# Layer norms cut into quarters and channels, a written order for the first attention, and other buffers for the weights of a four-layer network

## The chip, the cores and the metric

The kernel runs on one core of one Trainium2 chip. The metric is the device time of one execution in microseconds (us), taken as the median of several executions. The engines are TensorE (PE, matmuls; its weight loads are shown as PEld), VectorE (DVE), ScalarE (ACT), GpSimd (POOL), and SyncE (SP), which issues all DMA transfers of this kernel. Each engine runs its own instructions in one fixed order, and waits at an instruction until what it needs is there; whatever stands behind the waiting instruction waits too.

## What is computed

There are 8 sequences of 112 tokens with 512 channels (x), and 8 context sequences of 375 tokens. All arithmetic is fp32. Four layers follow each other:

```python
# layer 0: cross attention of one head, residual scaled by alpha
x = x + alpha * (softmax((x @ w_q.T) @ (ctx @ w_k.T).T / sqrt(512)) @ (ctx @ w_v.T)) @ w_o.T
# layers 1 and 2: a recurrent (RWKV) layer each
xa = layernorm(x); sx = previous_token(xa) - xa
w, k, v, r, g = five data-dependent mixes of xa and sx, times Wk, Wv, Wr, Wg and a decay
y = recurrence over the tokens, 32 heads of 16          # "time mix"
x = x + (groupnorm(y) * silu(g)) @ Wo.T
xc = layernorm(x); sxc = previous_token(xc) - xc        # "channel mix"
x = x + sigmoid((xc + sxc * m_r) @ Wfr.T) * (relu((xc + sxc * m_k) @ Wfk.T) ** 2 @ Wfv.T)
# layer 3: two cross attentions of 16 heads of 128, each behind a layernorm, then an MLP behind a layernorm
```

## The kernel before, in words

**Layout.** Activations are kept turned: the 512 channels as 4 chunks of 128 partitions, the 896 tokens along the free dimension, and worked on in two halves of 448 tokens (`h` = 0 and 1). One product of a 128x128 weight block with 448 tokens is two PE instructions in the profile; a projection of one half and one output chunk is 4 such products.

**Who sets the order.** The program is written in Tile, whose scheduler reorders the instructions of each engine; only in a block under `tc.manual_schedule` do PE, DVE, ACT and POOL keep the written order. Before, only the recurrence (L682) is such a block. DMAs all go through SP in one order.

**Layer 0** (L224 to L356). The attention is folded: `w_qk` = w_q turned times w_k turned, and `w_vo` = w_v turned times w_o (`product`, L296, whose output ACT copies out of PSUM at L305). Then for each of 8 sequences `b`: PE turns the context into `rows` (3 tiles, copied by DVE), makes the scores `sc` (L336), DVE and ACT make the softmax, PE turns the probabilities (`pt`, copied by DVE into `pts`), and multiplies (`av`). For every second sequence, `park` (L251) forms sums and differences of the two contexts that later layers use: DVE copies (L261) and POOL subtractions (L263) fill a tile, and five DMAs (L268) put 2.6 MB of it into DRAM. Contexts live in 4 buffers, so the later ones are loaded when earlier ones are done with. The output projection `ps_o` is added to x by DVE (L353).

**Between the layers.** `values()` (L823) is a generator of independent matmuls (`ps_vk`, L933: the value products of layer 3's attentions) that other code uses to fill PE while it waits: `fill(n)` takes n pieces of it. Its weights are loaded at the end of layer 0 (`wv`, L842), combined by POOL (L849 to L852), and DVE subtracts two biases (`over`, L979). Constants (`ones_t`, `pick`, `mean_h`, `less_mean_h`) are made just before layer 1 (L797 to L816).

**A layer norm** (`layer_norm_half`, L166) of one half: partial sums over the chunks by DVE (L178, L180), mean over channels by PE (L182), subtraction by DVE (L187), square by ACT (L189), partial sums and PE again for the variance, square root by ACT (L194), then on DVE one reciprocal of 128x448 (L195) and one multiplication of all 4 chunks, 128x1792 (L196), then 4 scalings by ACT (L202). There are 14 of these half norms. `fills` says how many pieces of filler are put behind the mean, the square and the variance.

**Layers 1 and 2.** Weights rotate through 4 buffers (`weight`, L124): a new weight's DMA starts once the last reader of the old one in its buffer is done. In the time mix the order of loading is Wg, Wv, Wk, Wr (`"gvkr"`); Wg and Wv are then reordered in place, half by half, by an ACT copy (L419, `turng`, `turnv`) and a DVE copy back (L420). The channel mix (L723) has one pool for its norm output, mixes, `kk` and `rr`; its three projections are `fk`, `fr` and `fv`; for `fv` DVE multiplies (L772) and POOL adds to x (L773).

**The way into layer 3.** The last channel mix runs its `fv` half by half, and starts the first norm of layer 3 for half 0 (`y_ln3`, without scaling) while half 1 is being multiplied. Layer 3 scales that half (L202) and norms half 1, with the first key projections as filler: `ps_k1k` and `ps_k5k` (L1166), which need the weight wk, sums of it by POOL (`wsk`, L1067 to L1070), and the parked tiles `cs`, `cx` and `cy` (loaded at L1221 to L1228).

Of the kernel before, what the change touches and what calls it, by code (L numbers as in the profile page):

```python
# [22 lines left out]
F32 = mybir.dt.float32  # L23
# [85 lines left out]
def tile_kernel(ctx: ExitStack, tc: tile.TileContext, d: dict, out: bass.AP):  # L109
# [26 lines left out]

    mean_c = const.tile([P, P], F32, name="mean_c")
# [28 lines left out]
    def layer_norm_half(ps, work, y, h, scale, offset, name, room=None, bank=None, fills=(2, 2, 4), small_tag="rstd"):  # L166
# [22 lines left out]
        nc.scalar.activation(sq, y, AF.Square)  # L189
        fill(fills[1])  # L190
        var = over_channels(sq, "var")
        fill(fills[2])
        rstd = small("rstd", "")
        nc.scalar.activation(rstd, var, AF.Sqrt, bias=eps)  # L194
        nc.vector.reciprocal(rstd, rstd)  # L195
        nc.vector.tensor_mul(y, y, rstd.unsqueeze(1).to_broadcast([P, NC, NH]))  # L196
        if scale is not None:
            scale_by_channel(y, y, scale, offset)
# [23 lines left out]


    def layer0():  # L224
# [3 lines left out]
        with (  # L228

            tc.tile_pool(name="a0s", bufs=2, space=PSUM) as ps2,  # L230
            tc.tile_pool(name="a0c", bufs=4) as near,
            tc.tile_pool(name="a0", bufs=1) as keep,
# [18 lines left out]
            def park(b, c1, c2):  # L251
# [7 lines left out]
                for k in range(2):  # L259
                    for y, z in ((b11, c11), (b21, c21), (b22, c22)):  # L260
                        nc.vector.tensor_copy(y[:, k], z[:, k])  # L261
                    for y, z, less in ((t0, c12, c11), (t1, c22, t0), (t2, c22, c12), (t3, c21, t1)):
                        nc.gpsimd.tensor_sub(y[:, k], z[:, k], less[:, k])  # L263
# [22 lines left out]
            def turned(w, name):  # L286

                t = keep.tile([P, NC, C], F32, tag="turned", bufs=3, name=f"t_{name}")
                for o in range(NC):
                    p = mm(ps, f"ps_t{name}_{o}")  # L290
                    for k in range(NC):
                        nc.tensor.transpose(p[:, k * P : (k + 1) * P], w[:, k, o * P : (o + 1) * P], ident)
                    (nc.vector.tensor_copy if o % 2 else nc.scalar.copy)(t[:, o, :], p)
                return t

            def product(a, b, name, pool, scale=1.0):  # L296

                y = pool.tile([P, NC, C], F32, tag=name, name=name)
# [9 lines left out]
            w_qk = product(turned(w_q, "q"), turned(w_k, "k"), "w_qk", keep, 1.0 / math.sqrt(C))  # L308
            q = keep.tile([P, NC, N], F32, name="q0")
            z = last.tile([P, NC, N], F32, name="z0")  # L310
            project(
                ps,
                w_qk,
                lambda k, h: halves(x[:, k, :], h),
                lambda o, h, p: nc.scalar.copy(halves(q[:, o, :], h), p),
                "q0",
            )
            w_vo = product(turned(w_v, "v"), w_o, "w_vo", last)
            for b in range(B):
                tok = slice(b * L, (b + 1) * L)  # L320
                if b + 1 < B:
                    context(b + 1)
                cx = cxs[b]
                if b % 2:
                    park(b, cxs.pop(b - 1), cxs.pop(b))
                rows = work.tile([CT, 3, C], F32, tag="rows", name=f"rows0_{b}")
                for t in range(3):
                    p = mm(ps, f"ps_r0_{b}_{t}")[:CT, :]
                    for k in range(NC):
                        nc.tensor.transpose(  # L330
                            p[:, k * P : (k + 1) * P], cx[:, k, t * CT : (t + 1) * CT], ident
                        )
                    nc.vector.tensor_copy(rows[:, t, :], p)
                sc = ps2.tile([L, S], F32, tag="sc", name=f"sc0_{b}")
                for k in range(NC):
                    nc.tensor.matmul(sc, q[:, k, tok], cx[:, k, :], start=k == 0, stop=k == NC - 1)  # L336
                prob = softmax(work, sc, S, f"0_{b}")
                pt = ps2.tile([CT, 3, L], F32, tag="pt", name=f"pt0_{b}")
                for t in range(3):
                    nc.tensor.transpose(pt[:, t, :], prob[:, t * CT : (t + 1) * CT], ident[:L, :L])  # L340
                pts = work.tile([CT, 3, L], F32, tag="pts", name=f"pts0_{b}")
                nc.vector.tensor_copy(pts, pt)
                av = ps2.tile([P, NC, L], F32, tag="av", name=f"av0_{b}")
                for o in range(NC):
                    for t in range(3):
                        nc.tensor.matmul(
                            av[:, o, :], rows[:, t, o * P : (o + 1) * P], pts[:, t, :], start=t == 0, stop=t == 2
                        )
                nc.scalar.copy(z[:, :, tok], av)
# [33 lines left out]
    def time_mix_inputs(n, pre, names, ones_t, first, k, v, r, g, decay, rows):  # L383
# [7 lines left out]
        with (  # L391
# [21 lines left out]
            ws = {f: weight(f"{pre}W{f}") for f in "gvkr"}  # L413
# [309 lines left out]
    def channel_mix(n, pre, names, first):  # L723
        nonlocal filler
        with (
            tc.tile_pool(name=f"c{n}", bufs=1) as one,
            tc.tile_pool(name=f"cw{n}", bufs=2) as work,
            tc.tile_pool(name=f"cp{n}", bufs=6, space=PSUM) as ps,
        ):
            f_k, f_r, f_v = (weight(pre + names[f]) for f in ("Fk", "Fr", "Fv"))  # L730
# [20 lines left out]
            kk = one.tile([P, NC, N], F32, name=f"kk{n}")  # L751
            rr = one.tile([P, NC, N], F32, name=f"rr{n}")
# [29 lines left out]
            else:  # L782
# [8 lines left out]
                layer_norm_half(ps, work, y, 0, None, None, "ln3_1", ([sq], None), None, (1, 1, 1))  # L791
# [4 lines left out]
    def rwkv_layers():  # L796
        with tc.tile_pool(name="rc", bufs=1) as one:  # L797
            ones_t = one.tile([P, P], F32, name="ones_t")
            mean_h = one.tile([P, P], F32, name="mean_h")
            less_mean_h = one.tile([P, P], F32, name="less_mean_h")  # L800
            center_h = less_mean_h, mean_h
            pick = one.tile([P, 4, 4 * HB], F32, name="pick")
            with tc.tile_pool(name="rs", bufs=1) as setup:
                heads = setup.tile([P, P + P + HS - 1], F32, name="heads")
                nc.sync.dma_start(heads, d["heads"])

                nc.vector.tensor_copy(ones_t.rearrange("p (q h r) -> p q h r", q=4, h=HB), turned(heads[:, :P]))
                same = setup.tile([P, P], F32, name="same")
                for q in range(4):
                    nc.sync.dma_start(same[32 * q : 32 * (q + 1)], turned_rows(d["heads"][:, :P], q))  # L810
                nc.scalar.mul(mean_h.rearrange("p (q h r) -> p q h r", q=4, h=HB), turned(same), 1.0 / HS)
                nc.vector.tensor_sub(less_mean_h, identity(setup, "rs"), mean_h)

                for r in range(4):
                    at = P + HS - 1 - 4 * r
                    nc.vector.tensor_copy(pick[:, r], heads[:, at : at + 16 * HB - 3 : 4])  # L816
            first = one.tile([P, 2, NC, B], F32, name="first")
            nc.sync.dma_start(first, d["first"])
            for n in (1, 2):
                rwkv(n, ones_t, center_h, pick, first)  # L820


    def values():  # L823
# [151 lines left out]
        for i in (1, 2):  # L975
# [3 lines left out]
            nc.vector.tensor_sub(over, over, bv)  # L979
# [219 lines left out]
    def attention(i, ident, h_in, work, kv, ps, ps2, keep, near, mlp_norm):  # L1199
# [61 lines left out]
        for h in range(2):  # L1261
            if i == 1 and not h:
                scale_by_channel(halves(h_in, 0), shared.pop("normed"), *scales)
            else:
                fill(2)
                layer_norm_half(ps, work, halves(h_in, h), h, *scales, f"ln3_{i}", room, ln_bank, (3, 3, 4))
# [276 lines left out]
```

## Time and profile before

| what | value |
|---|---|
| median of 3 runs | 2953.61 us (2950.38 to 2958.53) |
| profiled execution, its own time | 2960.41 us |
| its span in the trace | 2958.3 us, 2.1 us lie around it |
| granted PE clock, mean | 0.990 |
| PE busy | 2862.2 us |
| DVE, ACT, POOL busy | 1603.7, 1009.1, 872.6 us |
| DMA | 400.82 MB, mean 135 GB/s |

In the timelines that are shown, a row has the start in us, the duration in us, the engine, the line of the kernel, the operation, what it writes and reads (buffer numbers left out), the shape, how often it ran in a row, and in square brackets how long the engine stood idle before it and what ended that. In the tables of stretches, each engine has its busy time and its instructions, then follow the granted PE clock (1.00 is full), the share of the DMA engines' time and the GB/s. The chain of waits is the work that ended last, followed back through what released it.

### The profile page before, as it was taken

To read this page: it belongs to the slowest core of one execution; us is meant where nothing else is said; L and a number is where in the kernel's file an instruction comes from. 1 tells how busy PE (TensorE), PEld (TensorE's weight loads), DVE (VectorE), ACT (ScalarE), POOL (GpSimd) and SP (SyncE) were. 2 spreads that over 40 slices of the span, in tenths; PEclk is the share of its full clock that TensorE was granted. 3 is DMA by queue.
4 is the path that set the end of the run, shared out by engine and by line. 5 is a ranking of instruction groups with operands and counts; after the bars stand their busy time and mean duration, and the time that the engine had idled before them with its cause. 6 is when DMAs were issued, how large, how long until landed. Compare 5 with 4: busy or idle time off the path is not lost.

```text
span 2958.3 us, 29826 instructions
## 1 busy us (share of the span) xinstructions
PE 2862.2 (97%) x10130; PEld 1561.7 (53%) x10130; DVE 1603.7 (54%) x2350; ACT 1009.1 (34%) x2004; POOL 872.6 (29%) x700
## 2 busy tenths in 40 slices
PE   8989999999999999999899999999999999999999
PEld 4734443344444433356465656666565656656544
DVE  1564188856342788643455555545555554545455
ACT  2123466534243565532332323232331323323311
POOL 2332178744331687642411010100302010000030
PEclk9999999999999999999999999999999999999999
DMA  6521498943321989642344444334332433432110
GB/s 256 174 70 42 134 284 249 273 129 124 94 67 58 269 239 288 195 137 70 116 130 128 130 128 130 108 119 141 94 120 98 142 108 120 140 112 80 44 53 25
DMA packets 198743, 400.82 MB, mean 135 GB/s; under 512 B 33224, under 2 KB 119528, under 8 KB 191808
## 3 DMA queue, kind: packets, MB, share of 16 engines
q1 hardware_dynamic: 198592, 398.91, 43.3%
q8 instruction: 81, 1.33, 0.2%
q14 instruction: 70, 0.57, 0.1%
HBM read 321.06 MB, written 77.91 MB: 135 GB/s over the span
## 4 chain that ended last, share of the span: by engine, by line
PE 80%; DVE 7%; POOL 4%; DMA 3%; issue 3%; ACT 3%; SPq 0%; DVEq 0%; POOLq 0%; ACTq 0%
PE ps_vk L933 13%; PE ps_k1k L1166 10%; PE ps_k5k L1166 7%; PE av L1335 6%; PE sc L1322 5%; PE pt L1325 3%; PE ps_o L161 3%; PE ps_fk L161 2%; PE ps_k1q L1093 2%; PE ps_r L487 2%; PE ps_k L487 2%; PE ps_k7q L1093 2%; PE ps_fr L161 2%; PE ps_k5q L1093 2%; PE ps_k5o L1093 1%
## 5 line engine op out<-in xcount | busy, mean ns | idle before, releaser
L933 PE MATMUL ps_vk<-wv,cv 128*128 128x512 f32 x1296 | 583.7, 601 | 13.9 <-ACT k L1031 6.3
L933 PEld LDWEIGHTS ps_vk<-wv,cv 128*128 128x128 f32 x1296 | 244.0, 192 | 338.1 <-issue 287.9
L959 POOL TENSOR_TENSOR k<-k,k 128x512 f32<-128x512 f32 (+1 forms) x153 | 200.2, 1309 | 321.5 <-ACT k L958 264.3
L694 DVE TENSOR_TENSOR_SCAN st<-decay,kv 128x904 f32<-128x904 f32 x128 | 260.7, 2037 | 17.9 <-POOL rs L698 4.4
L698 POOL TENSOR_TENSOR rs<-st,r 128x896 f32<-128x896 f32 x128 | 247.0, 1929 | 53.3 <-DVE st L694 44.1
L218 ACT ACTIVATE prob<-sc,top 112x376 f32<-112x376 f32 (+1 forms) x264 | 151.8, 575 | 322.3 <-DVE top L215 194.8
L1322 PE MATMUL sc<-k,q 128*112 128x376 f32 x512 | 201.1, 485 | 0.7 <-ACT prob L218 0.7
L1335 PEld LDWEIGHTS av<-pts,v 125*128 125x128 f32 (+1 forms) x1536 | 185.0, 193 | 31.4 <-DVE pts L1331 16.6
L1315 POOL COPY k<-over_k 128x4 f32<-128x4 f32 x64 | 13.7, 223 | 605.0 <-PE sc L1322 577.0
L1335 PE MATMUL av<-pts,v 125*128 125x112 f32 (+1 forms) x1536 | 189.1, 277 | 2.1 <-DVE pts L1331 1.9
L1166 PE MATMUL ps_k1k<-cs,wsk 128*128 128x375 f32 x480 | 178.7, 481 | 1.5 <-ACT p1k L1169 1.5
L215 DVE TENSOR_REDUCE top<-sc 112x1 f32<-112x376 f32 (+1 forms) x264 | 143.3, 544 | 64.2 <-PE sc L1322 52.0
L690 DVE TENSOR_TENSOR kv<-vp,k 128x904 f32<-128x904 f32 x128 | 141.4, 1105 | 60.0 <-ACT vp L592 54.6
L958 ACT COPY k<-ps_vk 128x512 f32<-128x512 f32 (+1 forms) x153 | 89.1, 583 | 174.7 <-PE ps_vk L933 172.0
L1031 ACT COPY k<-ps_vk 128x512 f32<-128x512 f32 (+1 forms) x153 | 89.1, 582 | 163.2 <-PE ps_vk L933 156.0
L1325 PEld LDWEIGHTS pt<-ident_l,prob 112*125 112x125 f32 (+1 forms) x768 | 97.9, 177 | 73.2 <-DVE prob L220 44.2
L1325 PE MATMUL pt<-ident_l,prob 112*125 112x112 f32 (+1 forms) x768 | 121.4, 277 | 3.4 <-DVE prob L220 2.3
L220 DVE TENSOR_SCALAR prob<-prob,total 112x376 f32<-112x376 f32 (+1 forms) x264 | 119.7, 454 | 8.0
L1166 PEld LDWEIGHTS ps_k1k<-cs,wsk 128*128 128x128 f32 x480 | 89.7, 190 | 59.8 <-issue 2.1
L592 ACT COPY vp<-vj 128x896 f32<-128x896 f32 x124 | 112.8, 910 | 10.8 <-DMA vj<-rows 6.9
L1173 DVE TENSOR_TENSOR k<-ps_k5k,u2k 128x375 f32<-128x375 f32 x52 | 28.5, 548 | 159.2 <-PE ps_k5k L1166 158.2
L1342 DVE TENSOR_TENSOR ctxt<-av,bv 128x448 f32<-128x448 f32 x64 | 39.9, 624 | 127.3 <-PE av L1335 127.2
(389 smaller groups left out, 4820.6 us busy)
## 6 DMA issues: line engine op xcount, KB each, us to landing
vj<-rows SPq DMA_DIRECT2D x124, 448.0 KB
cv<-blocks SPq DMA_DIRECT2D x181, 251.5 KB
cs<-blocks SPq DMA_DIRECT2D x120, 375.0 KB
wvs<-k SPq DMA_DIRECT2D x128, 256.0 KB
v<-wvs SPq DMA_DIRECT2D x64, 512.0 KB
cx<-in_ctxT SPq DMA_DIRECT2D x38, 750.0 KB
v<-wvs SPq DMA_DIRECT2D x64, 252.0 KB
wvs<-k SPq DMA_DIRECT2D x64, 224.0 KB
```

The costliest lines, as they stand in the source:

```text
L161: nc.tensor.matmul(p, w[:, k, o * P : (o + 1) * P], rhs(k, h), start=k == 0, stop=k == NC - 1)
L215: nc.vector.tensor_reduce(top, scores, AX.X, ALU.max, negate=True)
L218: nc.scalar.activation(prob, scores, AF.Exp, bias=top, accum_out=total)
L694: nc.vector.tensor_tensor_scan(flat(st), flat(decay[:, c]), flat(kv), 0.0, ALU.mult, ALU.add)
L698: nc.gpsimd.tensor_mul(by_batch(rs), st[:, :, :L], by_batch(r[:, c, :]))
L933: nc.tensor.matmul(to, left, right, start=start and n == 0, stop=k == 1, skip_group_check=True)
L959: nc.gpsimd.tensor_add(y, z, y)
L1093: nc.tensor.matmul(to, lhsT, rhs, start=start and k == 0, stop=k == 1, skip_group_check=not start)
L1166: nc.tensor.matmul(y, lhsT, rhs, start=start and k == 0, stop=k == 1, skip_group_check=True)
L1322: nc.tensor.matmul(sc, q[:, o, tok], kt[:, o, :], start=True, stop=True)
L1325: nc.tensor.transpose(pt[t][:nt, o, :], prob[:, t0 : t0 + nt], ident[:L, :L])
L1335: nc.tensor.matmul(av[:, o, :], v[:nt, t, o * HD : (o + 1) * HD], pts[:nt, t, o, :], start=t == 0, stop=t == 2,)
```

## The change

Six things change, all in the order and size of the steps; what is computed stays.

1. **Norms**: in `layer_norm_half` the reciprocal is made in four quarters of 112 tokens, and the multiplication in four chunks of 448. All 14 half norms take this form.
2. **The split last norm**: with `hold`, the norm of half 0 at the end of layer 2 keeps its standard deviation in `sq[:, 0]` and returns a generator; its reciprocals and multiplications are taken by `next(beside)` inside the norm of half 1, and the scaling of half 0 comes behind that norm.
3. **Layer 0 in the written order**: everything from `w_qk` to the last `av` is under `manual_schedule`. A sequence's softmax lies beside the turning of the next one's context. Contexts have 6 buffers, and five of them are loaded ahead; the copies of `park` go from DVE to ACT; `park(1)` comes behind the first scores; the turned w_v and w_qk live in the weight buffers.
4. **Constants** are made in layer 0 (`patterns`), just behind `w_vo`, no longer before layer 1.
5. **`over`**: the two bias subtractions go from DVE to POOL, where they stand behind the four combinations of `wv`.
6. **Buffers**: the time mixes load their weights in the order Wk, Wg, Wr, Wv. The channel mixes have two pools, `lower` and `upper`, and the two layers use them the other way round.

The changed program has 2410 DVE instructions for 2352 (in the program's own count), 1766 ACT for 1742, and the same on PE (5536), POOL (705) and SP (1301).

```diff
@@ layer_norm_half
-        rstd = small("rstd", "")
+        next(beside, None)
+        rstd = sq[:, 0] if hold else small("rstd", "")
         nc.scalar.activation(rstd, var, AF.Sqrt, bias=eps)
-        nc.vector.reciprocal(rstd, rstd)
-        nc.vector.tensor_mul(y, y, rstd.unsqueeze(1).to_broadcast([P, NC, NH]))
-        if scale is not None:
-            scale_by_channel(y, y, scale, offset)
+        def scaled():
+            for q in range(4):
+                part = slice(q * NH // 4, (q + 1) * NH // 4)
+                nc.vector.reciprocal(rstd[:, part], rstd[:, part])
+            yield
+            for c in range(NC):
+                nc.vector.tensor_mul(y[:, c], y[:, c], rstd)
+            if scale is not None:
+                scale_by_channel(y, y, scale, offset)
+            yield
+        if hold:
+            return scaled()
+        for _ in scaled():
+            pass
@@ layer0
-            tc.tile_pool(name="a0c", bufs=4) as near,
+            tc.tile_pool(name="a0c", bufs=6) as near,
...
-                        nc.vector.tensor_copy(y[:, k], z[:, k])
+                        nc.scalar.copy(y[:, k], z[:, k])
...
+            for b in range(1, 6):
+                context(b)
+            made = patterns(keep, ident)
+            next(made)
...
+            with tc.manual_schedule(engines=ORDERED):
+                w_qk = product(turned(w_q, "q"), turned(w_k, "k"), "w_qk", wpool, "w", 1.0 / math.sqrt(C))
...
+                w_vo = product(turned(w_v, "v", wpool, "w"), w_o, "w_vo", last, "w_vo")
+                next(made)
+                rows, sc = scores(0, lambda: None)
+                park(1, cxs[0], cxs[1])
+                prob = normalized(*exponentials(0, sc))
+                for b in range(B):
+                    if b in (1, 2):
+                        context(b + 5)
...
+                    left = rows
+                    if b + 1 < B:
+                        rows, sc = scores(b + 1, transposes)
+                        prob, total = exponentials(b + 1, sc)
...
+                    if b in (1, 3, 5):
+                        park(b + 2, cxs[b + 1], cxs[b + 2])
+                    if b + 1 < B:
+                        normalized(prob, total)
...
@@ time_mix_inputs
-            ws = {f: weight(f"{pre}W{f}") for f in "gvkr"}
+            ws = {f: weight(f"{pre}W{f}") for f in "kgrv"}
@@ channel_mix
-            tc.tile_pool(name=f"c{n}", bufs=1) as one,
+            tc.tile_pool(name=f"c{n}", bufs=1) as lower,
+            tc.tile_pool(name=f"cc{n}", bufs=1) as upper,
...
+            one, late = (lower, upper) if n == 2 else (upper, lower)
...
-            kk = one.tile([P, NC, N], F32, name=f"kk{n}")
-            rr = one.tile([P, NC, N], F32, name=f"rr{n}")
+            kk = late.tile([P, NC, N], F32, name=f"kk{n}")
+            rr = late.tile([P, NC, N], F32, name=f"rr{n}")
...
-                layer_norm_half(ps, work, y, 0, None, None, "ln3_1", ([sq], None), None, (1, 1, 1))
+                shared["rest"] = layer_norm_half(
+                    ps, work, y, 0, None, None, "ln3_1", ([sq], None), None, (1, 1, 1), hold=True
+                )
@@ values
-            nc.vector.tensor_sub(over, over, bv)
+            nc.gpsimd.tensor_sub(over, over, bv)
@@ attention
             if i == 1 and not h:
+                rest = shared.pop("rest")
+                continue
+            fill(2)
+            layer_norm_half(..., (3, 3, 4), beside=rest if i == 1 else iter(()))
+            if i == 1:
                 scale_by_channel(halves(h_in, 0), shared.pop("normed"), *scales)
```

## The prediction

> **What bounds the kernel.** I read the page first, then listed the stretches in which PE stands idle or runs at a lower clock, then the timelines of the engines around each of them that the change touches.
>
> ```profile
> PE 2862.2 (97%) x10130; PEld 1561.7 (53%) x10130; DVE 1603.7 (54%) x2350; ACT 1009.1 (34%) x2004; POOL 872.6 (29%) x700
> ...
> PE 80%; DVE 7%; POOL 4%; DMA 3%; issue 3%; ACT 3%; SPq 0%; DVEq 0%; POOLq 0%; ACTq 0%
> ```
>
> PE is the bound: 2958.3 - 2862.2 = 96 us is all that it stands idle, and the change takes no matmul away. So it can gain from two things only: idle gaps, and the stretches at half clock that follow gaps. The table of stretches shows those near the change (columns: PE, PEld, DVE, ACT, POOL, granted clock, DMA share, GB/s):
>
> ```profile
> 64.00:71.00 7.00, 5.76 (x7) 2.52 (x8) 1.16 (x2) 1.67 (x3) 0.00 (x0) 0.52 0.04 18
> 153.00:156.50 3.50, 3.50 (x6) 1.52 (x5) 0.44 (x2) 0.31 (x1) 0.00 (x0) 0.52 0.71 192
> 699.00:702.50 3.50, 2.90 (x4) 1.50 (x5) 3.39 (x4) 0.79 (x1) 3.50 (x5) 0.52 0.83 272
> 1429.50:1436.50 7.00, 5.14 (x8) 2.42 (x9) 2.65 (x2) 2.76 (x7) 6.92 (x8) 0.51 0.84 263
> 1439.70:1443.30 3.60, 3.27 (x6) 1.89 (x7) 2.35 (x3) 0.39 (x1) 1.80 (x2) 0.53 0.68 229
> ```
>
> At a clock of 0.52 a stretch of d us loses 0.48 d: 3.4, 1.7, 1.7, 3.4 and 1.7 us, 11.9 in all.
>
> **Layer 0, `w_vo`.** PE's timeline, then ACT's:
>
> ```profile
> 65.24 10.01 PE L302 MATMUL ps_w_vo<-w_L_xattn_w_o_None,t_v 128*128 128x512 f32 x16 [3.27 <-ACT w_vo L305]
> ```
> ```profile
> 62.70 1.99 ACT L419 COPY turnv<-w_L_xattn_Wv_None 128x1024 f32<-128x1024 f32 x2 [8.04 <-DMA w_L_xattn_Wv_None<-in_L_xattn_Wv]
> ```
>
> ACT stands at layer 1's `turnv`, which waits for a DMA issued at 53.77, with the copy of `w_vo` behind it and PE behind that. In the changed program's order `w_vo` 0 comes first, then a turn of Wg. Its load is issued when PE has turned w_v (about 54.4), behind Wk's, and two loads of 1 MB at the 5.1 us that such a load took (730.97 to 736.07 for Wv) end by 60 to 65; `w_vo` 3 is due at 65.4. The gap of 3.27 and the half clock go: -6.6 us. If Wg comes late, the same wait stands one output later (0).
>
> **Layer 0, the attention.** PE waits 2.66 us at 100.21 for `pts`: DVE stands at a `park` copy whose context is still on its way. Contexts are now loaded ahead and the copies (24 of 0.53 us) go to ACT, idle there for most of the time: -2.7. New is what stands behind these copies on ACT: the next exponential. A copy waits for the previous park to land, as the tile has one buffer. One cycle is 8 POOL subtractions (7.4 us) plus the tail of the puts; a pair of sequences is 13.9 us of PE, so a tail of 6 us is hidden. The new order also makes DVE write Wv back in the fourth sequence, ahead of `rows` and `pts`, and Wv's load now stands on SP behind the puts of the second park: between 0 and 4 us, I take 1.5, since it lands within about 2 us of its use by the load time above. Together -1.2 (-2.7 to +2).
>
> **Between layers 0 and 1.** DVE's timeline, then PE's:
>
> ```profile
> 142.68 2.73 DVE L180 TENSOR_TENSOR part_mean_ln<-part_mean_ln,x 128x448 f32<-128x448 f32 x1
> 145.33 5.58 DVE L979 TENSOR_TENSOR over<-over,bv 4x512 f32<-4x512 f32 x2
> 150.84 0.67 DVE L353 SCALAR_TENSOR_TENSOR x<-ps_o,alpha,x 128x448 f32<-128x448 f32 x1
> ```
> ```profile
> 151.56 10.98 PE L161 MATMUL ps_o<-z,w_vo 128*128 128x448 f32 x24 [3.63 <-DVE x L353]
> ```
>
> While POOL combines `wv` (139.9 to 150.4), a DVE addition that takes 0.62 us elsewhere took 2.73, and the two tiny `over` 5.58. With `over` on POOL and the constants made earlier, DVE has one 0.68 and one slow sum per 3.0 us of PE; the slow sum remains, and the PSUM buffers absorb its 0.4 us. Gap and half clock go: -5.3 (-2 if the sums still hold up PE). On POOL `over` has only SP's small puts behind it, which nobody wants soon.
>
> **Norms.** L624's reciprocal of 128x224 takes 1.52 us and L195's of 128x448 2.95: 6.4 ns per element and 0.10 fixed, so a quarter of 112 takes 0.81. Four take 3.24 (+0.29), four multiplications of 0.62 take 2.48 instead of 2.02 (+0.46). DVE pays 0.75 per half norm, 10.5 for 14, beside PE. But ACT's first scaling starts after 3.24 + 0.62 = 3.86 instead of 4.97, and its four of 0.68 follow: the chain gets 1.1 us shorter. [...] The chain ends in a gap at few norms: layer 1's first (1.28 us at 181 to 186, -0.7), the channel mix of layer 1 (0.86 for the second mean and 2.54 at 697.06 for `xk`, of which about 1.8 go, also because `turng` leaves ACT there, and with them the 1.7 of half clock), that of layer 2 (2.50 at 1308.52, -0.5), layer 3's other norms (-1). That is -0.7 - 4.0 - 0.5 - 1 = -6.2; the scheduler also pulled a filler product (0.87 us) ahead at some of these, so I take -5 (-8 to 0).
>
> **Weight order, start of layer 2.** This is a new wait. SP's timeline, then ACT's:
>
> ```profile
> 730.97 0.35 SPq L127 DMA_DIRECT2D w_L_xattn_Wv_None<-in_L_xattn_Wv x1
> ...
> 779.08 0.33 SPq L127 DMA_DIRECT2D w_L_xattn_Wr_None<-in_L_xattn_Wr x1
> ```
> ```profile
> 783.14 1.70 ACT L189 ACTIVATE sq_ln<-xa 128x1792 f32<-128x1792 f32 x1 [0.80 <-DVE xa L187]
> ```
>
> Now the weight of 779.08, free only after `fv`'s last product, is Wv. It lands 5.1 us later, at 784.2, and in the changed order its two turning copies (1.04 each, with DVE's 0.69 beside) stand ahead of this square, DVE's ahead of the variance sums. The square moves from 783.1 to about 786.9, the variance with it; PE has 0.9 to 1.8 us more filler there: +2.5 (0, if the copies find a gap, to +6 with a half clock behind it).
>
> **Way into layer 3.** DVE, then PE:
>
> ```profile
> 1423.37 2.94 DVE L195 RECIPROCAL rstd__ln<-rstd__ln 128x448 f32<-128x448 f32 x1
> ...
> 1426.71 2.01 DVE L196 TENSOR_TENSOR y_ln<-y_ln,rstd__ln 128x1792 f32<-128x1792 f32 x1
> 1429.74 0.62 DVE L180 TENSOR_TENSOR t_h<-t_h,x 128x448 f32<-128x448 f32 x1 [1.02 <-POOL x L773]
> ```
> ```profile
> 1430.51 1.83 PE L182 MATMUL mean_ln<-t_h,mean_c 128*128 128x448 f32 x2 [4.12 <-DVE t_h L180]
> ...
> 1433.19 2.84 PE L1166 MATMUL ps_k5k<-cs,wsk 128*128 128x375 f32 x4 [0.85 <-DMA cs<-blocks]
> ...
> 1440.04 2.84 PE L1166 MATMUL ps_k5k<-cy,wsk 128*128 128x375 f32 x4 [2.50 <-DMA cy<-in_ctxT]
> ```
>
> The last addition to x comes behind a whole reciprocal and beside the multiplication (it takes POOL 2.83 us instead of 1.13), and the loads of `cs` (1429.73) and `cy` wait for it. With 1.30 at 1456.49, gaps are 8.8 and half clock 5.1: 13.9. Now the parked loads need only `fr`'s last product (1398), wk follows once the first has landed, and 3.7 MB end by about 1415 at the 230 to 260 GB/s of those rows; PE wants them at 1425. What is late next: POOL makes `wsk` (4 of 1.27) ahead of the last addition, which ends at 1428.8; the mean then starts at 1429.6, with 2.5 key blocks of 1.26 done before it from 1424.96, a gap of 1.5. Later `wo` and `wq` (2 MB) stand on SP ahead of the next pair's loads: 1 to 2.5. So -10 (-4 to -13).
>
> **Sum.** -6.6 - 1.2 - 5.3 - 5 + 2.5 - 10 = -25.6. On the profiled 2960.4 that is 2934.8; the profiled run stands 6.8 above the median, so **2928**.
>
> The clock is the largest doubt. [...] In the trace half clock also came behind gaps of 2.50 and 2.54, and none behind 2.66 or 2.37. [...] I keep the rows, but gaps of 1.5 to 3 that remain can bring a stretch back.
>
> **Rivals.** (a) *Half clock stays, or shifts*: gaps close, but the 11.9 us return behind shorter ones: 2940. For it: stretches behind 2.5; against: most gaps vanish wholly. (b) *The waits only change places*: Wg lands after `w_vo` 3 (0), the parks cost 2, Wv costs 5, the mean in layer 3 still waits for POOL and only 4 are won there: 0 + 2 - 5.3 - 2 + 5 - 4 = -4.3, which is 2949. For it: the new waits are real in the order; against: each has slack by the durations above. (c) *Slower, by the park cycle*: if the puts' tail is long, each of three cycles holds ACT, with it the exponential and PE. The gain of the rest is 24.4, so from (24.4 / 3) = 8.1 us over 13.9, a cycle of 22, it loses; that is 14.6 us behind POOL's work for 2.69 MB, 184 GB/s without overlap. Stretches of 4 us there moved 157 to 313 GB/s, the better ones at a full queue, so a cycle of 11 to 14 is likelier. At 26 us the time is 2954 + 12 = 2966. (d) The scheduler undoing the written order is excluded: the order of the built program has it.
>
> **Chances.** 0.45 for 2928, 0.29 for (a), 0.14 for (b), 0.12 for (c). A measurement tells about 0.3%, 9 us, from no change: faster 0.73, same 0.16, slower 0.11. The range reaches from near all best ends (2914) to just beyond (b), 2950.
>
> **What would show it.** No gap over 1 us in `w_vo`, none at `ps_o`; `cs` issued right behind `fr`, and the first query product, at 1467.11 before, some 24 us earlier, near 1443; a gap of 2 to 4 us at layer 2's first variance. Wrong it would be if ACT stood at `park` copies for DMA, if PE's clock fell below 0.990, or if the filler pulled ahead left gaps later.

## Result: 0.4% faster, under half of the forecast, and the profile after

| what | before | after |
|---|---|---|
| median of 20 runs | 2956.38 us (2950.38 to 2967.76) | 2947.77 us (2937.66 to 2952.57) |
| ratio, 95% interval | | 0.9959, 0.9948 to 0.9969 |
| profiled execution, span, granted clock | 2960.41, 2958.3, 0.990 | 2940.07, 2938.3, 0.996 |
| PE idle in the span | 96 us | 90 us |

The change makes the kernel about 12 us faster by the ratio (0.41%, 0.31 to 0.52%). The forecast was 25.6 us, 0.87%. The measured median lies in the range; the direction was right, the size was not. The page of the kernel after, engines and chain of waits:

```profile
PE 2848.3 (97%) x10130; PEld 1555.3 (53%) x10130; DVE 1605.4 (55%) x2408; ACT 1020.6 (35%) x2028; POOL 870.8 (30%) x700
PE 83%; DVE 9%; ACT 3%; POOL 3%; issue 2%; DMA 1%; DVEq 0%; POOLq 0%; ACTq 0%; SPq 0%
```

PE is still the bound. In the chain, DMA and POOL together have lost 3 points, and PE has gained 3. PE's busy time is 14 us less for the same matmuls, which is mostly the clock: 0.996 in this execution, 0.990 in that of before. That flatters it: over 20 timed runs of each the mean granted clock was 0.9893 before and 0.9923 after. The two profiled executions differ by 20.1 us between the first and the last matmul, and a second pair, taken later, by 2.5. No single pair measures this change.

The stretches that answer to four of those of before, in the same columns:

```profile
64.00:71.00 7.00, 6.75 (x23) 3.54 (x22) 1.50 (x7) 2.99 (x8) 0.00 (x0) 1.00 0.20 44
147.00:154.00 7.00, 7.00 (x19) 3.23 (x17) 2.05 (x3) 0.00 (x0) 3.17 (x5) 1.00 0.33 77
687.00:694.00 7.00, 6.41 (x15) 2.88 (x16) 6.82 (x5) 1.28 (x3) 7.00 (x8) 1.00 0.18 72
1417.00:1424.00 7.00, 3.80 (x11) 1.62 (x9) 5.02 (x5) 1.99 (x4) 6.87 (x8) 1.00 0.29 121
```

The clock is 1.00 in all four. At `w_vo` and `ps_o` PE is busy nearly throughout. On the way into layer 3 (the last row) it is busy for only 3.80 of 7.00 us: the half clock has gone there, the idle time has not.

To see where the time went, the trace was cut at fixed matmuls (the first of a named product to the first of the next). "Before" is the mean of two profiles, "after" the mean over the profiles of all kernels that leave that stretch as the change has it (those with another order of weights, whole norms, a joined norm or one pool are left out where their edit falls into the stretch):

| stretch | before | after | difference | forecast |
|---|---|---|---|---|
| start to the first `rows` (`w_vo`) | 67.7 | 62.3 | -5.4 | -6.6 |
| layer 0's attention | 55.65 | 55.05 | -0.6 | -1.2 |
| `ps_o` to layer 1's first mean | 31.6 | 27.85 | -3.8 | -5.3 |
| layer 1's time mix | 500.2 | 498.8 | -1.4 | -0.7 |
| channel mix of layer 1 | 116.4 | 116.55 | +0.15 | -4.0 |
| start of layer 2 | 105.9 | 107.7 | +1.8 | +2.5 |
| channel mix of layer 2 | 133.1 | 133.6 | +0.6 | -0.5 |
| first key product to first query product of layer 3 | 40.6 | 36.2 | -4.3 | -10 |
| from there to the end | 1483.9 | 1486.2 | +2.3 | -1 |

With -0.2 in the rest of layer 2 the sum is -10.9, which lies within the interval of the ratio (9 to 15 us). The two profiles of after differ by up to 3.7 us in a row and by 7.8 in the last, so that a difference of under 1 us in a single row says little. In the forecast's column the norms still count -6.2, before its allowance of 1.2. Three rows make most of the miss: the channel mix of layer 1 (4.2), the way into layer 3 (5.7), the end (3.3).

### The profile page after: what moved, and what is told of

Read it like the earlier page. It is cut to its first block, busy times and chain, and to the rows that moved or that the text cites. A ratio compares the mean times of both kernels' runs of the same rounds, so it can differ in the third digit from the quotient of the medians.

```text
span 2938.3 us, 29915 instructions
## 1 busy us (share of the span) xinstructions
PE 2848.3 (97%) x10130; PEld 1555.3 (53%) x10130; DVE 1605.4 (55%) x2408; ACT 1020.6 (35%) x2028; POOL 870.8 (30%) x700
## 4 chain that ended last, share of the span: by engine, by line
PE 83%; DVE 9%; ACT 3%; POOL 3%; issue 2%; DMA 1%; DVEq 0%; POOLq 0%; ACTq 0%; SPq 0%
PE ps_vk L1001 13%; PE ps_k1k L1234 10%; PE ps_k5k L1234 7%; PE av L1416 6%; PE sc L1403 5%; PE ps_o L163 3%; PE pt L1406 3%; PE ps_fk L163 2%; PE ps_k1q L1161 2%; PE ps_r L569 2%; PE ps_k L569 2%; PE ps_k5q L1161 2%; PE ps_fr L163 2%; PE ps_v L569 2%; PE ps_k7q L1161 2%
## 5 line engine op out<-in xcount | busy, mean ns | idle before, releaser
L235 ACT ACTIVATE prob<-sc,top 112x376 f32<-112x376 f32 x256 | 147.2, 575 | 296.3 <-DVE top L232 168.0
L232 DVE TENSOR_REDUCE top<-sc 112x1 f32<-112x376 f32 x256 | 139.0, 544 | 53.7 <-PE sc L1403 49.0
L237 DVE TENSOR_SCALAR prob<-prob,total 112x376 f32<-112x376 f32 x256 | 113.4, 443 | 7.7
```

What stands on the lines that cost most here:

```text
L235: nc.scalar.activation(prob, scores, AF.Exp, bias=top, accum_out=total)
```

## Experiments

"Ratio" is the time over that of the kernel before, with its 95% interval. Diffs are against the kernel after unless another base is named.

**The two kernels again.** No edit; this shows what one profile can tell.

> The kernel before, unchanged, for a second profile and for its clock in each timed run. Theory A (half clock comes by chance): PE's idle time is that of the first profile within 1 us (90.1 us in gaps over 0.3 us), as the program is the same, but the stretches at half clock, 30.7 us of loss in the first profile, lie at partly other gaps, and their loss differs by several us. Theory B (the stretches belong to their gaps): the same stretches at 64, 153, 699, 1430 and 1440 us. Ratio 1.000 within its interval by both.

> The changed kernel again. Theory A: idle 82 us in gaps over 0.3 us as in its first profile, but a loss to half clock nearer 20 us than the 12 of that profile, at other gaps; time 0.996 of before, that is idle -8 and half clock -2. Theory B: again 12 us of loss and a time near 0.993.

Measured: before 2955.78 us, ratio 0.9999 (0.9986 to 1.0012); after 2944.36 us, ratio 0.9966 (0.9954 to 0.9978). Between the two profiles of before, the half clock cost 30.7 and 25.6 us, and at partly different gaps. Between those of after it cost 12.0 and 23.9. The wait of `cy` (2.50 us, with a half clock behind it) is missing in the second profile of before. A product that waited 2.54 us ahead of the half clock in the table of before is followed by the full clock in the second profile (PE's timeline, then the stretch):

```profile
696.32 1.02 PE L161 MATMUL ps_fk<-xk,w_L_xattn_fWk_None 128*128 128x448 f32 x2 [2.55 <-DVE xk L741]
```
```profile
696.00:699.50 3.50, 3.18 (x8) 1.36 (x8) 3.39 (x4) 0.90 (x2) 3.50 (x4) 1.00 0.75 243
```

The same wait, 2.55 us, and a clock of 1.00 instead of 0.52: half clock behind such a gap is a matter of chance from run to run.

**Wv third, Wr last.** Tests the new wait at the start of layer 2, and whether Wv was late in layer 0.

```diff
-            ws = {f: weight(f"{pre}W{f}") for f in "kgrv"}
+            ws = {f: weight(f"{pre}W{f}") for f in "kgvr"}
```

> Weights loaded in the order k, g, v, r, so that Wv and not Wr is third. Theory: the gap of 2.68 us at pts in layer 0 (DVE stands at the copy back of Wv) and the gap of 1.15 us at layer 2's start come from Wv's place; both go, idle falls by 3 to 4 us against the changed kernel, to about 79. Rival: in layer 0 ACT waits for the puts of the park before (1.92 us), so a gap of 1 to 2 us stays at the same place, without Wv.

Measured: 2941.42 us, ratio 0.9957 (0.9945 to 0.997). In the kernel after, ACT's timeline and then PE's show the wait:

```profile
772.18 1.99 ACT L501 COPY turnv<-w_L_xattn_Wv_None 128x1024 f32<-128x1024 f32 x2 [1.58 <-DMA w_L_xattn_Wv_None<-in_L_xattn_Wv]
774.08 0.58 ACT L1099 COPY k<-ps_vk 128x512 f32<-128x512 f32 x1
774.55 1.70 ACT L191 ACTIVATE sq_ln<-xa 128x1792 f32<-128x1792 f32 x1
```
```profile
774.71 4.05 PE L1001 MATMUL ps_vk<-wv,cv 128*128 128x512 f32 x8 [1.15 <-ACT k L1099]
779.27 1.02 PE L184 MATMUL var_ln<-part_var_ln,mean_c 128*128 128x448 f32 x2 [0.50 <-DVE part_var_ln L182]
```

ACT stands at `turnv`, as the forecast said; but the first to suffer is the filler, whose copy `k` stands behind `turnv`, not the variance. With Wv third the copies are out of the way and the square starts 3.2 us behind the mean instead of 6.4:

```profile
768.63 1.70 ACT L191 ACTIVATE sq_ln<-xa 128x1792 f32<-128x1792 f32 x1 [0.67 <-DVE xa L189]
```

Idle time in this stretch falls from 5.7 and 6.0 to 3.95 us: the order of the weights costs about 1.9. In layer 0 the theory holds too: the wait for `pts` that the first profile of after shows at 105.11 (2.68 us) is there in all seven profiles with Wr third, 0.65 to 2.68 us, and in neither of the two with Wv third (this run and the last one below), though ACT stood 0.73 us at the park copies here as well. The whole run is not distinguishable from the kernel after.

**Whole reciprocal and multiplication again.** All norms.

```diff
-            for q in range(4):
-                part = slice(q * NH // 4, (q + 1) * NH // 4)
-                nc.vector.reciprocal(rstd[:, part], rstd[:, part])
+            nc.vector.reciprocal(rstd, rstd)
...
-            for c in range(NC):
-                nc.vector.tensor_mul(y[:, c], y[:, c], rstd)
+            nc.vector.tensor_mul(y, y, rstd.unsqueeze(1).to_broadcast([P, NC, NH]))
```

> The changed kernel with one whole reciprocal and one whole multiplication per half norm. Theory: the shorter chain of the quarters was spent by the scheduler, which puts fewer filler products behind the variance (16 matmuls instead of 20 ahead of fk), so in layers 1 and 2 idle changes by less than 1.5 us in all; only at the way into layer 3 the last addition to x waits again for a whole reciprocal, 1 to 2 us. Rival (as predicted): idle is 3 to 5 us more in the norms alone.

Measured: 2944.69 us, ratio 0.997 (0.9958 to 0.9982): not distinguishable from the kernel after. Mean to `fk` in layer 1's channel mix takes 36.72 us instead of 35.35, but the stretch behind it gives it back. PE has 20 filler matmuls there again, and the gap ahead of `fk` is 2.55 us. The 1 to 2 us expected on the way into layer 3 did not come (36.26 us). The stretch at the end has 7.74 us idle instead of 9.70 and 11.07.

**The first half's norm in one piece.** `hold=True` goes, and with it the generator: that half's reciprocal and multiplication come before the norm of the other half.

```diff
-                shared["rest"] = layer_norm_half(
-                    ps, work, y, 0, None, None, "ln3_1", ([sq], None), None, (1, 1, 1), hold=True
-                )
+                layer_norm_half(ps, work, y, 0, None, None, "ln3_1", ([sq], None), None, (1, 1, 1))
...
```

> The changed kernel with the split norm joined again: half 0's reciprocals (quarters), multiplications (chunks) and scalings stand as before the change. Theory: splitting it is worth 3 to 4 us on the stretch from the first key product to the first query product, so that stretch, 36.2 us in both profiles of the changed kernel, becomes 39 to 40 here. Rival (as predicted): the split is worth the whole 10 us, and the stretch becomes 44 to 46. Rival 2: the earlier loads (cs, wk) alone brought the gain, and it stays 36.

Measured: 2944.83 us, ratio 0.9963 (0.9949 to 0.9977). First key to first query product takes 36.65 us (5.28 idle, 1.71 by half clock) against 36.2. The split norm is worth nothing that can be measured; what is gained on the way into layer 3 is gained without it.

**One pool in the channel mixes.**

```diff
-            tc.tile_pool(name=f"cc{n}", bufs=1) as upper,
...
-            one, late = (lower, upper) if n == 2 else (upper, lower)
+            one = late = lower
```

> The changed kernel with one pool for each channel mix, as before. Theory: the two pools are what lets the parked loads for layer 3 start behind fr (1387.8 in the changed kernel) and the maa loads of layer 2 behind fr (743.3); with one pool they start behind the last addition to x, and the stretch from the first key to the first query product is 3 to 6 us longer than 36.2, with waits for cs and cy. Rival: the split norm alone made that gain, and the stretch stays within 1 us.

Measured: 2951.18 us, ratio 0.9981 (0.9969 to 0.9993). The stretch takes 40.28 us, as before the change. PE's timeline:

```profile
1420.91 2.84 PE L1233 MATMUL ps_k5k<-cs,wsk 128*128 128x375 f32 x4 [3.02 <-DMA cs<-blocks]
```

The loads of `cs` are issued at 1416.13 here, and at 1387.76 in the kernel after. The second pool is what frees them, and is worth 4.1 us.

**The kernel before, with two pools alone.**

```diff
-            tc.tile_pool(name=f"c{n}", bufs=1) as one,
+            tc.tile_pool(name=f"c{n}", bufs=1) as lower,
+            tc.tile_pool(name=f"cc{n}", bufs=1) as upper,
...
+            one, late = (lower, upper) if n == 2 else (upper, lower)
...
-            kk = one.tile([P, NC, N], F32, name=f"kk{n}")
-            rr = one.tile([P, NC, N], F32, name=f"rr{n}")
+            kk = late.tile([P, NC, N], F32, name=f"kk{n}")
+            rr = late.tile([P, NC, N], F32, name=f"rr{n}")
```

> The kernel before with only the two pools of the channel mix. Theory: the parked loads start behind fr, the waits for cs and cy (0.7 to 3.4 us, and a stretch at half clock) go, and the stretch from the first key to the first query product falls from 39.0 to 42.1 to about 36.5; the wait of 4.12 us for the last addition to x becomes shorter, as in the joined norm of the changed kernel. Rival: that wait stays (the loads were hidden behind it), and the stretch is 39 to 40.

Measured: 2950.66 us, ratio 0.9983 (0.9972 to 0.9995). The stretch takes 34.73 us with 4.42 idle, less than in the kernel after (36.2 with 6.4). So nothing else in the change helps there, and the quarters and the split seem to cost up to 1.5 us (one profile; the joined norm's 36.65 us, less the 1.71 of half clock in it, points the same way).

**The first half's scalings on POOL.** Tests whether ACT's scalings make the gaps of 1.81 us on the way into layer 3.

```diff
-                scale_by_channel(halves(h_in, 0), shared.pop("normed"), *scales)
+                normed = shared.pop("normed")
+                for c in range(NC):
+                    nc.gpsimd.tensor_scalar(
+                        halves(h_in, 0)[:, c, :], normed[:, c, :], column(scales[0], c), column(scales[1], c), ALU.mult, ALU.add
+                    )
```

> The changed kernel with the scalings of half 0 before layer 3 (4 of 128x448) on POOL instead of ACT. Theory: the copy of u2k stands on ACT behind two of them, which wait for DVE; the gap of 1.81 us ahead of the third key product goes, and the stretch from the first key to the first query product falls from 36.2 to about 34.5. Rival: PE then waits as long for the mean's or the variance's sums (1.02 us at the variance grows), and the stretch stays within 0.7 us.

Measured: 2944.31 us, ratio 0.9959 (0.9946 to 0.9973). The gap at `u2k` is gone, but the variance waits longer, 2.42 us for 1.02, and `u3k` still waits:

```profile
1436.50 1.57 PE L184 MATMUL var_ln<-t_h,mean_c 128*128 128x448 f32 x2 [2.42 <-DVE t_h L182]
1446.50 1.53 PE L1234 MATMUL ps_k1k<-cs,w_L_xattn_wk 128*128 128x375 f32 x4 [1.00 <-ACT u3k L1237]
```

The stretch takes 36.87 us (5.70 idle, 1.71 by half clock): the wait changes place. The variance starts 16.2 us behind the first key product, in the kernel after 16.5. So the norm's chain on DVE, not the scaling alone, sets the time here.

**`over` on DVE again.**

```diff
-            nc.gpsimd.tensor_sub(over, over, bv)
+            nc.vector.tensor_sub(over, over, bv)
```

> The changed kernel with the two bias subtractions on DVE again. Theory: they alone make the stall in the output projection of layer 0, so the stretch from its first product to the first mean, 27.9 us in four profiles of changed kernels, becomes 30 to 33 us (29.9 and 33.4 in two profiles of the kernel before); idle +1.5 to +3.6 us. Rival: the constants moved to layer 0 did it, and the stretch stays within 0.5 us.

Measured: 2948.76 us, ratio 0.9982 (0.9973 to 0.999). The stretch from `ps_o` takes 32.47 us instead of 27.85:

```profile
144.15 10.72 PE L163 MATMUL ps_o<-z,w_vo 128*128 128x448 f32 x24 [2.91 <-DVE x L435]
```

**The kernel before, with `over` on POOL alone.** The same line the other way round.

```diff
-            nc.vector.tensor_sub(over, over, bv)
+            nc.gpsimd.tensor_sub(over, over, bv)
```

> The kernel before with only the two bias subtractions on POOL. Theory: the stretch of the output projection of layer 0 falls from 29.8 to 33.4 to 27.9 us at most 28.5, 2 to 5 us less, and the rest stays; ratio 0.9985 to 0.999. Rival: the constants, which stay on DVE there, and the slow sum hold it as long, and the stretch stays above 29.5.

Measured: 2956.43 us, ratio 1.0005 (0.9993 to 1.0017), nothing gained. DVE's timeline, then PE's:

```profile
158.37 0.29 DVE L812 TENSOR_TENSOR less_mean_h<-ident_rs,mean_h 128x128 f32<-128x128 f32 x1 [7.81 <-ACT mean_h L811]
```
```profile
159.31 3.35 PE L161 MATMUL ps_o<-z,w_vo 128*128 128x448 f32 x4 [4.77 <-DVE x L353]
```

DVE now stands at a constant, `less_mean_h`, with the additions to x behind it. The constant waits for ACT and ACT for the loads of `same`, which stand on SP behind the puts of `over`; these wait for POOL (2.47 us of subtractions from 152.14). So each half of this edit needs the other: `over` on POOL and the constants made earlier give 27.85 us together, the first alone in the kernel before 35.36, the second without the first 32.47.

**The kernel before, with quarters and chunks alone.** The edit of the norms without `hold`.

```diff
-        nc.vector.reciprocal(rstd, rstd)
-        nc.vector.tensor_mul(y, y, rstd.unsqueeze(1).to_broadcast([P, NC, NH]))
+        for q in range(4):
+            part = slice(q * NH // 4, (q + 1) * NH // 4)
+            nc.vector.reciprocal(rstd[:, part], rstd[:, part])
+        for c in range(NC):
+            nc.vector.tensor_mul(y[:, c], y[:, c], rstd)
```

> The kernel before with only quarters and chunks in its 14 half norms. Theory: idle within 2 us of the kernel before (83 to 90), 1 to 2 us less in layers 1 and 2 and 2 us more behind the MLP's norms; ratio 0.999 to 1.0005. Rival (as predicted): 5 us faster, a ratio of 0.998.

Measured: 2957.03 us, ratio 1.0000 (0.999 to 1.0011). The quarters alone are worth nothing. Between variance and `fk` in layer 1's channel mix there are 16 filler matmuls and a gap of 2.79 us, as in the kernel after. At the end of the program, idle time rises to 10.82 us (8.59 and 7.32 in the profiles of before).

**The version put together from these.** Wv third, and the last norm, in front of the MLP, with the whole reciprocal and multiplication; all else as after.

```diff
+            if name == "ln_mlp":
+                nc.vector.reciprocal(rstd, rstd)
+                nc.vector.tensor_mul(y, y, rstd.unsqueeze(1).to_broadcast([P, NC, NH]))
+            else:
...
-            ws = {f: weight(f"{pre}W{f}") for f in "kgrv"}
+            ws = {f: weight(f"{pre}W{f}") for f in "kgvr"}
```

> The changed kernel with the loading order k, g, v, r, and with whole reciprocals and multiplications in the two norms ahead of the MLP only. Theory: the first takes away about 1.8 us of idle at layer 2's start, the second about 2 us of the gaps behind that norm (0.56 at u3k, 1.28 instead of 0.71 at sc); idle near 75 us, time 3 to 4 us under the changed kernel, a ratio near 0.9950 to the kernel before. Rival: the gaps move elsewhere, and the ratio is that of the changed kernel, 0.996 to 0.9965.

Measured: 2936.63 us (2934.59 to 2943.32), ratio 0.9939 (0.9922 to 0.9957), the lowest median of all. Its interval overlaps that of the kernel after (0.9948 to 0.9969) slightly, so six runs do not settle how much it gains on it. The end of the kernel after, and then this one's, on PE:

```profile
2710.55 1.53 PE L1234 MATMUL ps_k1k<-cs,w_L_xattn_wk 128*128 128x375 f32 x4 [0.56 <-ACT u3k L1237]
2725.17 0.89 PE L1403 MATMUL sc<-k,q 128*112 128x376 f32 x2 [1.28 <-ACT prob L235]
2729.03 0.57 PE L1406 MATMUL pt<-ident_l,prob 112*125 112x112 f32 x3 [0.56 <-DVE prob L237]
```
```profile
2721.21 0.89 PE L1407 MATMUL sc<-k,q 128*112 128x376 f32 x2 [0.71 <-ACT prob L239]
```

With the whole norm the waits of `ps_k1k` and `pt` are gone and that of `sc` is 0.71 instead of 1.28. The last stretch has 8.19 us idle, where the quarters have 9.4 to 11.4.

## Why the forecast was wrong in size, step by step

The steps that failed are three terms of the sum: the norms (-5, about 0 measured), the way into layer 3 (-10, -4.3 measured), and, across both, the half clock credited in full from one execution. That 2947.77 lies close to rival (b)'s 2949 is luck: of the steps in which it differs from the forecast only one came true as a whole, 4 us on the way into layer 3.

**Layer 0, `w_vo`: right, a little too large.** The gap is gone in every profile of the new order. The term was -6.6 and measured -5.4. The half clock of 3.4 us behind it was credited in full; in the second profile of before there was none there, and the stretch was 2.5 us shorter.

**The attention and its parks: right.** -0.6 for -1.2, with a spread of 54.1 to 57.8 us. The first park cycle took 16.5 to 16.7 us in all profiles, the next two 15.7 and 16.2 in the first profile of after (the copies start at 85.80, 101.48 and 117.68) and 13.7 to 14.8 in the others, rather than 11 to 14. The mechanism of the slower rival is real, but small. ACT's timeline after, in the first profile:

```profile
101.48 2.54 ACT L296 COPY blocks<-cx 128x375 f32<-128x375 f32 x6 [1.92 <-DMA blocks<-blocks]
...
104.35 1.99 ACT L501 COPY turnv<-w_L_xattn_Wv_None 128x1024 f32<-128x1024 f32 x2
```

The puts of the park before it hold ACT for 1.92 us; `turnv` stands behind these copies, DVE's write-back behind `turnv`, and `pts` behind that: PE waits 2.68 us. In the second profile the same copies start at 98.80 without a wait, and PE waits 0.65. The seven waits average 1.4 us for 1.5 forecast; but Wv's load, which the forecast feared, was not late (`turnv` starts with no wait for it): its place on ACT and DVE makes the wait, as the run with Wv third shows. From 22 us per cycle, by the forecast's own estimate, it would have lost, and no profile comes near.

**Between the layers: right, too large by 1.5.** All idle time went. The credit of 5.3 was the first profile of before; the second has 1.53 us of idle and no half clock there. The step "on POOL `over` has only SP's small puts behind it, which nobody wants soon" is true of the changed kernel only, because the constants have moved: in the kernel before they stood behind those puts.

**Norms: -5 was wrong, it is about 0**, as the run with them alone shows (1.0000). "The chain gets 1.1 us shorter" holds: in layer 1's channel mix `fk` starts 10.7 us behind the variance, 12.1 before. But that does not close the gap. PE's timeline before, then after:

```profile
687.46 1.02 PE L182 MATMUL var_ln<-part_var_ln,mean_c 128*128 128x448 f32 x2
688.31 8.75 PE L933 MATMUL ps_vk<-wv,cv 128*128 128x512 f32 x20
699.60 1.86 PE L161 MATMUL ps_fk<-xk,w_L_xattn_fWk_None 128*128 128x448 f32 x2 [2.54 <-DVE xk L741]
```
```profile
676.91 1.02 PE L184 MATMUL var_ln<-part_var_ln,mean_c 128*128 128x448 f32 x2 [0.50 <-DVE part_var_ln L182]
677.77 7.03 PE L1001 MATMUL ps_vk<-wv,cv 128*128 128x512 f32 x16
687.59 1.02 PE L163 MATMUL ps_fk<-xk,w_L_xattn_fWk_None 128*128 128x448 f32 x2 [2.79 <-DMA cv<-blocks]
```

Before, 20 filler matmuls (8.75 us) stood between the variance and `fk`; now 16 (7.03). The chain became 1.4 us shorter and the filler 1.7, so the gap grew from 2.54 to 2.79. (The row puts it down to a DMA; the same gap of 2.79 in the second profile is put down to DVE's `xk`. It waits for several things that end close together.) Those 4 matmuls run later, where PE would have been busy anyway. The forecast saw that the scheduler moves filler and took 1.2 off for it; it is the whole gain. The two runs that change the norms alone, in either direction, show the same pair: 16 matmuls and 2.79 us with quarters, 20 and 2.55 without.

At the end of the program the quarters cost idle time, most of the +2.3, but hardly by the added DVE time that the forecast weighed (0.75 us per half norm). DVE's timeline at the last norm, after and then in the version with it whole:

```profile
2705.04 2.98 DVE L204 RECIPROCAL t_mlp<-t_mlp 128x112 f32<-128x112 f32 x4
2708.75 0.62 DVE L1423 TENSOR_TENSOR ctxt<-av,bv 128x448 f32<-128x448 f32 x1 [0.73 <-PE av L1416]
2709.29 2.22 DVE L207 TENSOR_TENSOR h_in<-h_in,t_mlp 128x448 f32<-128x448 f32 x4
2711.43 0.54 DVE L1241 TENSOR_TENSOR k<-ps_k5k,u2k 128x375 f32<-128x375 f32 x1
```
```profile
2701.97 2.94 DVE L203 RECIPROCAL t_mlp<-t_mlp 128x448 f32<-128x448 f32 x1
2704.83 0.48 DVE L1245 TENSOR_TENSOR k<-ps_k5k,u2k 128x375 f32<-128x375 f32 x1
2705.24 2.01 DVE L204 TENSOR_TENSOR h_in<-h_in,t_mlp 128x1792 f32<-128x1792 f32 x1
2707.16 0.62 DVE L1427 TENSOR_TENSOR ctxt<-av,bv 128x448 f32<-128x448 f32 x1
```

The norm's own work on DVE is only 0.25 us longer (2.98 + 2.22 for 2.94 + 2.01). What differs is the order that the scheduler made: with quarters the addition to `ctxt`, which waits for PE, stands ahead of the multiplications, and the `k` that empties a key product's PSUM stands behind them. It also puts no score product `sc` early any more, so that ACT's table load of 1.28 us for the softmax, hidden before (at 2735.32 in the kernel before, behind an early `sc`), comes at 2723.16 with PE waiting. So "beside PE", where the forecast put DVE's added time, fails at the last norm: by these rows DVE's order reaches PE there. That whole tiles there take these waits away is shown by the version with it whole; that the +2.3 is all of this is not, since single gaps there (1.36 or 2.42 at `ps_k6fc`) vary between executions of one kernel.

**Start of layer 2: right**, +1.8 for +2.5, one instruction away from where it was put: it is the filler's copy that waits behind `turnv`.

**Way into layer 3: -10 was wrong, it is -4.3.** Right were the early loads, and POOL's sums ahead of the last addition: `cs` was issued at 1387.76, just behind `fr`, and the mean waits 1.80 us for 1.5 forecast. What the sum left out beside them is the norm's chain on DVE and what stands behind it on ACT. PE's timeline after, then ACT's:

```profile
1419.72 0.99 PE L184 MATMUL mean_ln<-t_h,mean_c 128*128 128x448 f32 x2 [1.80 <-DVE t_h L182]
...
1424.42 1.53 PE L1234 MATMUL ps_k1k<-cs,wsk 128*128 128x375 f32 x4 [1.81 <-ACT u2k L1237]
...
1431.10 0.99 PE L184 MATMUL var_ln<-t_h,mean_c 128*128 128x448 f32 x2 [1.02 <-DVE t_h L182]
...
1440.21 1.53 PE L1234 MATMUL ps_k1k<-cs,w_L_xattn_wk 128*128 128x375 f32 x4 [1.81 <-ACT u3k L1237]
```
```profile
1421.64 0.76 ACT L219 ACTIVATE h_in<-y_ln,scaled 128x448 f32<-128x448 f32 x1 [3.84 <-DVE y_ln L207]
1423.25 0.76 ACT L219 ACTIVATE h_in<-y_ln,scaled 128x448 f32<-128x448 f32 x1 [0.85 <-DVE y_ln L207]
1423.91 0.45 ACT L1237 COPY u2k<-ps_k1k 128x375 f32<-128x375 f32 x1
```

The scalings of half 0 moved onto ACT ahead of the copies that empty PSUM for the key products, and they wait for DVE's multiplications; with the scalings on POOL PE waits for DVE's sums instead (2.42 us ahead of the variance). So the four gaps sum to 6.44 us where the forecast left 2.5 to 4; that is 2.4 to 3.9 of the missing 5.7. A further 1.6 is the baseline: before had 42.14 us in the profile that the forecast used and 38.98 in the other, mean 40.6. Some 1 us was counted twice, since the half clock of 1429.5 to 1436.5 lay in part over the gaps. And the gain is due to the two pools, not to the split norm.

**The clock: the doubt was right, the sum ignored it.** The forecast credited 11.9 us, gap by gap, from one execution. What decides can be read off the granted clock. In each of 14 profiles all half-clock stretches begin at one and the same phase of a period of 3.413 us and last 1, 2 or 3 periods (3.4, 6.8, 10.2 us); the phase differs from execution to execution. Cut into windows of this period (from 45 us on), full clock is followed by half clock so often:

| PE idle within one window | followed by half clock |
|---|---|
| 2.0 us or more | 60 of 60 windows |
| 1.6 to 2.0 us | 19 of 70 |
| under 1.6 us | 50 of some 11,500: 42 at three places of layers 1 and 2, 5 at the program's end, 3 others |

With 1.9 us as the limit, which is an estimate between 1.6 and 2.0, a gap of 2.54 us drops the clock only where the grid leaves some 1.9 us of it in one window: at (3.41 - 1.9) + (2.54 - 1.9) = 2.15 of 3.41 us of phase, 63%. One of 4.12 always does by the same estimate, and did in both profiles of before (clock 0.51 from 1429.5 to 1436.5, and 0.50 from 1428 to 1435 in the second); and short gaps can do it together: in the second profile of after, gaps of 1.55 and 1.15 us with 2.2 us of idle time in the window that ends at 2701.18 did. Sliding the grid over the idle gaps of the two profiles of each kernel, with this limit, gives an estimate of 6 to 7 us less loss after. The runs agree: time lost to the clock, (1 - clock) x span, is 31.6 us before and 22.7 after. That is about 9 us less. So half clock did fall, but by less than the 11.9 credited, and partly into time in which PE stood idle.

## What to carry to other kernels

Before crediting a shorter chain, look at what fills the wait: where a scheduler places filler work, it can spend the gain by placing less, and cutting one step into parts can make it place other steps elsewhere, so compare the order of both programs at each place that counts. When loads or buffers stop being late, sum the chain of every engine that comes next, the PSUM-emptying copies included. Price half clock behind a gap as a probability (15 of 30 here for gaps of 2.4 to 3.0 us), never as the loss that one execution shows, and profile both kernels at least twice before explaining a difference under 1%.

## What the hardware showed that was not expected

In these traces the clock follows a fixed grid: PE idle time of 2.0 us or more within one window of 3.413 us was followed by half clock in 60 of 60 windows. A single gap can fall into one window or be divided between two: in the first profile of before, the 2.54 us at 697.06 had 2.05 of them in one window and half clock behind, the 2.66 us at 100.21 had 1.57 and 1.10 in two and full clock. In six of the profiles (before and after, their repeats, Wv third, whole norms), gaps of 2.4 to 3.0 us were followed by half clock in 15 of 30 cases. Several short ones count together, as those of 1.55 and 1.15 us in the second profile of after. Three places in layers 1 and 2 (near 188, 277 and 894 us in after), with hardly any idle time (0.24, 0.65 and 0.26 us in the window ahead, in that profile), lost the clock in all 14 profiles; why is open, no run was made on it.
